# A planned graph layer on TensorE: one broadcast planned as a longer transfer, and new due times for the steps of three stages

## The chip, the cores and the metric

The kernel runs on one core of one Trainium2 chip. The metric is the device time in microseconds (us). The core's engines are TensorE (PE; its weight loads are PEld), VectorE (DVE), ScalarE (ACT), GpSimd (POOL) and SyncE (SP), which here issues every DMA. Each runs its own instructions in order and waits on semaphores for the others.

## The reference

For 64 graphs of 256 nodes and width 768, with an integer adjacency matrix per graph:

```
h   = relu(layernorm(x))
ctx = adj @ (h Wadj + badj) / deg + adj^T @ (h Wrev + brev) / rdeg + h Wself + bself
rel = sum_j adj E[adj] Wr + br deg + sum_j adj^T E[reversed adj] Wrr + brr rdeg
out = x + ctx + rel
```

All is float32.

## The kernel before

A graph (called batch here) is two halves of 128 nodes, c = 0 and 1. Three 768x768 weights times h are nine block products of 256-wide pieces; they are computed with 15 combined products after the manner of fast matrix multiplication, the left side being pieces of h ("a0" to "b2") and sums of them, the right side sums of weight blocks. To keep float32 accuracy each side is split into reduced-precision words, and a product is three passes of four matmuls of 128x384, collected in PSUM tiles (chains y, z, w in sweep one; x, v, u, t in sweep two), with a scaling by ACT between passes.

Not all right-hand words fit in SBUF at once, so the work has stages. The **opening** treats batch 0 with plain float32 matmuls ("whole", L795) while the right-hand words of sweep one are made. **Sweep one** runs 8 products for each of 62 batches and stores the partial blocks and h to DRAM. The **change** treats batch 63 with "whole" and makes the words of sweep two. **Sweep two** reloads, runs the other 7 products and the aggregation by adj ("agg", L925) and stores the result.

In sweep one each batch starts with `front1`: load x and its transposed copy xt (one tile per half, L692, L694); take means and variances (`stats`, `aggr`, `eps`, `pow`); transpose the four statistics columns into a small tile, `line` (L728); store that to DRAM, `d` (L733); read it back broadcast to all partitions, `row` (L740, 128 partitions of 2 KB, 256 KB written); then for each half `centre` on POOL (L754, h minus the row of means) and `norm` on DVE (L758, relu and scale). `norm` reads two SBUF operands. The products' left words come next (L566 to L583), and then the matmuls (L594).

The order of instructions on each engine is no loop: a planner (`Plan.schedule`) simulates the engines when the program is built. Each step has an engine, a planned duration and a due time (`rank`): the batch's start r plus a fixed number plus an entry of the table `OFFSETS`. A step is never due before a step that it needs. Among the steps that are ready in the simulation, each engine takes the one that is due first. A step's kind in the table carries "@" for batch 0, "@1" for batch 1, "$" for batch 63, "$1" for batch 62, and nothing for all others, so an entry without a mark acts on sixty batches. A DMA is planned on one queue as size/330 us, and its landing later by a constant:

```
LANDS = {"load": 2.2, "store": 1.5}
...
def on_queue(kb):
    return kb / 330.0
```

The size given for `row` was 400, so the plan has 400/330 + 2.2 = 3.41 us from issue to landing when the queue is free. Steps with `lock=True` (POOL's elementwise steps, `norm`, some of DVE's) are planned so that no POOL step and no such DVE step run together. On the chip nothing of this simulation remains but the order of each engine's instructions and the semaphores between them.

Of the kernel before, what the change touches and what calls it, by code (L numbers as in the profile page):

```python
# [102 lines left out]
    "bias adj": -238.9, "bias forward": 39.45, "bias rev": -3.35, "bias rev again": 15.06, "bias reverse": 37.57,  # L103
    "bias self": 30.03, "bias self again": 9.91, "bias01": 24.14, "bias01$1": -41.79, "bias01@1": 36.62,
# [10 lines left out]
    "degree@1": -1.22, "double adj": 35.08, "double own": -49.23, "eT": -24.29, "eps": 4.28, "eps$": 7.22,  # L115
# [1138 lines left out]
```

## Time and profile before

| | |
|---|---|
| median of 3 runs | 2445.14 us (2444.12 to 2447.47) |
| the profiled execution | 2447.47 us |
| its span, first to last instruction | 2445.7 us |
| mean granted TensorE clock | 0.999 |
| PE busy in the span | 2411.1 us (99%) |
| DVE, ACT, POOL busy | 87%, 85%, 58% |

The profiled execution is one of the three runs. Its time lies 1.8 us above its span. The page's times are from the span's start. "Idle before" is the time that an engine stood still ahead of an instruction, with what released it. A matmul's busy time overlaps that of the next one, so the number of matmuls begun in a stretch says more about PE's pace than its busy share.

### The profile page before, as it was taken

How to read it: one execution, taken by the hardware profiler on the slowest of the kernel's cores; microseconds unless marked ns; L12 is line 12 of the kernel's file. 1: busy time of each engine (PE TensorE's matmuls, PEld its weight loads, DVE VectorE, ACT ScalarE, POOL GpSimd, SP SyncE). 2: the span in 40 equal slices, each digit the busy share in tenths (PEclk: the TensorE clock that was granted, in tenths of full speed). 3: DMA queues.
4: the chain of work that ended last, by engine and by line, in shares of the span. 5: the costliest groups of instructions: out<-in, count | busy, mean ns of one | idle time of the engine just before them, and what ended most of it. 6: DMA issues, size and time to landing. Idle time of an engine off the chain costs nothing.

```text
span 2445.7 us, 43188 instructions
## 1 busy us (share of the span) xinstructions
PE 2411.1 (99%) x13510; PEld 2346.0 (96%) x13510; DVE 2133.7 (87%) x3953; ACT 2088.5 (85%) x3936; POOL 1409.2 (58%) x1230
## 2 busy tenths in 40 slices
PE   7999999999999999999999999999999999999998
PEld 4999999999999999997899999999999999999998
DVE  6888898898988889885889888888888888889888
ACT  7888888888888888888888888888888888888887
POOL 7666666666666666564555555555555555555554
PEclk9999999999999999999999999999999999999999
DMA  7788888877888888877666666666666666666664
GB/s 266 269 270 278 261 275 269 274 275 267 272 269 277 277 268 275 273 260 254 208 221 225 224 225 220 223 220 220 220 220 223 223 220 220 220 220 219 222 223 154
DMA packets 225543, 593.03 MB, mean 242 GB/s; under 512 B 25116, under 2 KB 25116, under 8 KB 225308
## 3 DMA queue, kind: packets, MB, share of 16 engines
q1 hardware_dynamic: 225308, 590.22, 71.3%
q8 instruction: 108, 1.77, 0.3%
q14 instruction: 127, 1.04, 0.1%
HBM read 366.65 MB, written 223.48 MB: 241 GB/s over the span
## 4 chain that ended last, share of the span: by engine, by line
PE 53%; ACT 1%; DVE 0%; issue 0%; DVEq 0%; ACTq 0%
PE x L594 21%; PE agg L925 14%; PE v L594 5%; PE t L594 5%; PE u L594 5%; PE whole L795 2%; PE y L594 0%; ACT agg L933 0%; PE w L594 0%; PE pr L850 0%; ACT copy L517 0%; DVE c L676 0%; PE z L594 0%; DVE c L674 0%; ACT a L893 0%
## 5 line engine op out<-in xcount | busy, mean ns | idle before, releaser
L913 POOL TENSOR_TENSOR hl<-c,hl 128x768 fp32r<-128x768 f32 x256 | 470.8, 1850 | 552.1 <-ACT hl L909 306.1
L594 PE MATMUL x<-word,left 128*128 128x384 f32 x2976 | 577.9, 335 | 1.3 <-ACT x L647 0.9
L594 PE MATMUL y<-word,left 128*128 128x384 f32 x2976 | 569.7, 335 | 1.7 <-ACT y L647 0.7
L594 PEld LDWEIGHTS y<-word,left 128*128 128x128 f32 x2976 | 519.9, 188 | 5.5 <-ACT y L647 1.7
L594 PEld LDWEIGHTS x<-word,left 128*128 128x128 f32 x2976 | 520.3, 188 | 4.5 <-ACT x L647 1.2
L925 PE MATMUL agg<-hl,a 128*128 128x384 f32 x2048 | 399.5, 337 | 4.3 <-ACT agg L933 4.3
L925 PEld LDWEIGHTS agg<-hl,a 128*128 128x128 f32 x2048 | 360.0, 188 | 5.9 <-ACT agg L933 5.2
L754 POOL TENSOR_TENSOR h<-h,row 128x768 f32<-128x768 f32 x126 | 230.2, 1848 | 151.5 <-DMA kept<-x 41.1
L594 PE MATMUL z<-word,left 128*128 128x384 f32 x1488 | 304.2, 339 | 6.0 <-ACT c L665 5.1
L594 PE MATMUL w<-word,left 128*128 128x384 f32 x1488 | 299.7, 335 | 1.3 <-DVE word L531 1.2
L594 PEld LDWEIGHTS z<-word,left 128*128 128x128 f32 x1488 | 256.0, 188 | 21.6 <-ACT c L665 17.0
L594 PEld LDWEIGHTS w<-word,left 128*128 128x128 f32 x1488 | 262.0, 188 | 3.3 <-ACT top L573 1.8
L943 DVE SCALAR_TENSOR_TENSOR c<-agg,rd,c 128x768 f32<-128x768 f32 x252 | 254.5, 1011 | 3.1 <-PE agg L925 2.2
L647 ACT ACTIVATE y<-y 128x768 f32<-128x768 f32 x248 | 195.4, 788 | 55.9 <-PE y L594 55.8
L647 ACT ACTIVATE x<-x 128x768 f32<-128x768 f32 x248 | 191.3, 793 | 27.5 <-PE x L594 26.9
L909 ACT ACTIVATE hl<-c 128x768 fp32r<-128x768 f32 x256 | 213.8, 837 | 1.0 <-DVE c L676 0.8
L573 ACT ACTIVATE top<-left 128x256 f32<-128x256 f32 x496 | 179.6, 379 | 39.2 <-DVE left L583 38.8
L583 DVE SCALAR_TENSOR_TENSOR left<-left,top 128x256 fp32r<-128x256 f32 x496 | 193.9, 410 | 2.3
L933 ACT ACTIVATE agg<-row_forward,sqd 128x768 f32<-128x768 f32 x128 | 115.4, 902 | 84.8 <-DVE c L674 84.8
L583 DVE SCALAR_TENSOR_TENSOR left<-left 128x256 fp32r<-128x256 f32 x434 | 183.5, 434 | 0.0
L676 DVE SCALAR_TENSOR_TENSOR c<-x,c 128x768 f32<-128x768 f32 x124 | 118.1, 953 | 70.2 <-ACT agg L933 68.5
L758 DVE SCALAR_TENSOR_TENSOR h<-h,row 128x768 f32<-128x768 f32 x126 | 157.8, 1253 | 0.0
(127 smaller groups left out, 4619.2 us busy)
## 6 DMA issues: line engine op xcount, KB each, us to landing
c<-kept SPq DMA_DIRECT2D x316, 384.0 KB
kept<-c SPq DMA_DIRECT2D x252, 384.0 KB
x<-in_x_dram SPq DMA_DIRECT2D x128, 384.0 KB
h<-in_x_t_dram SPq DMA_DIRECT2D x128, 384.0 KB
out_dram<-c SPq DMA_DIRECT2D x126, 384.0 KB
kept_h<-h SPq DMA_DIRECT2D x124, 384.0 KB
h<-kept_h SPq DMA_DIRECT2D x124, 384.0 KB
adj<-in_adj_dram SPq DMA_DIRECT2D x64, 512.0 KB
```

What stands on the lines that cost most here:

```text
L573: lambda: nc.scalar.activation(view(top), t(w)[:, 0].bitcast(F32), AF.Copy),
L583: lambda: nc.vector.scalar_tensor_tensor(t(w)[:, 2], t(w)[:, 1].bitcast(F32), -STEP, first(), op0=ALU.mult, op1=ALU.add), s == 1,
L594: nc.tensor.matmul(t(q)[:, half, : H // 2], t(w)[:, lw, f, :], t(r[rw])[:, f, ts(half, H // 2)], start=start and i == 0 and f == 0, stop=s ...
L647: lambda: nc.scalar.activation(view(), view(), AF.Copy, scale=scale),
L676: emit = lambda to=to, sign=sign: nc.vector.scalar_tensor_tensor(to(), view(), sign * UP, to(), op0=ALU.mult, op1=ALU.add)
L754: lambda h=h, one=one, engine=engine: engine.tensor_tensor(t(h), t(h), one(0), op=ALU.subtract),
L758: lambda h=h, one=one: nc.vector.scalar_tensor_tensor(t(h), t(h), 0.0, one(1), op0=ALU.max, op1=ALU.mult), b != 0 or part is not None,
L909: lambda: nc.scalar.activation(t(pair)[:, 0], t(o), AF.Copy, scale=LOWER),
L913: lambda: nc.gpsimd.tensor_tensor(t(pair)[:, 1], t(o), t(pair)[:, 0].bitcast(F32), op=ALU.subtract),
L925: nc.tensor.matmul(t(q)[:, half, : H // 2], t(s["a"])[:, c, k, ts(ic, P)], t(pairs[c])[:, part, ts(half, H // 2)], start=False, stop=(c == ...
L933: lambda q=q, ic=ic, row=row: nc.scalar.activation(t(q)[:, :, : H // 2], t(row).rearrange("p (k n) -> p k n", k=2), AF.Copy, scale=t(sqd)[ ...
L943: lambda q=q, to=to, ic=ic: nc.vector.scalar_tensor_tensor(to(), t(q)[:, :, : H // 2], t(rd)[:, ic, k : k + 1], to(), op0=ALU.mult, op1=AL ...
```

## The change

One number in `front1` changes: the transfer `row` is planned with 560 in place of 400 (1.70 us on the queue in place of 1.21, and 3.90 us to the landing in place of 3.41). The transfer itself stays as it is. And 523 of the 821 entries of `OFFSETS` change: 216 without a mark, 94 each of "@1" and "$1", 67 of "$" and 52 of "@". They belong to the opening, to sweep one and to the change; the entries of sweep two's products, reloads and aggregation keep their values, except those of batch 63. No instruction is added, removed or altered; all that differs is the order on each engine. The new entries were found by a search in which planned transfers land late at random. Of the diff's lines these hold the entries spoken of below:

```diff
--- before.py
+++ after.py
...
-    "c11@": 32.1, "c11@1": -1.29, "c12": 22.01, "c12$1": 29.3, "c12@": -4.98, "c12@1": 18.89, "centre0": 4.08,
...
-    "centre0$": 31.91, "centre0$1": -227.73, "centre0@": -27.75, "centre0@1": -14.15, "centre1": 6.08,
...
-    "copy of 6": -106.6, "copy of 7": 34.39, "copy of 8": -14.49, "copy of 9": -4.54, "d": -0.46, "d$": -31.64,
...
-    "left2 8@1": -28.68, "left2 9": 7.17, "left2 9$1": 9.22, "left2 9@1": -124.24, "less": 35.53, "line": 18.08,
...
-    "load raw11.1": -125.08, "load raw12.0": -1.16, "load raw12.1": -347.46, "load raw20.0": -341.35,
...
-    "low12@": -65.09, "low12@1": -2.48, "more": -34.88, "norm0": 19.03, "norm0$": -217.44, "norm0$1": -38.93,
-    "norm0@": 43.2, "norm0@1": -11.82, "norm1": -62.27, "norm1$": 17.96, "norm1$1": 29.72, "norm1@": 37.5,
...
-    "right2": 29.95, "right3": 33.09, "right4": -0.47, "right6": -45.6, "right8": -31.54, "row": 0.71, "row$": 4.41,
...
-    "x0$": 0.9, "x0$1": -71.15, "x0@": -629.88, "x0@1": -16.01, "x1": -0.52, "x1$": 2.98, "x1$1": -6.07,
-    "x1@": -413.86, "x1@1": 25.42, "xt0": 19.12, "xt0$": -1.32, "xt0$1": 18.27, "xt0@": -172.07, "xt0@1": 17.01,
-    "xt1": 9.96, "xt1$": 14.9, "xt1$1": 16.79, "xt1@": -25.36, "xt1@1": 22.17,
...
+    "c11@1": -1.29, "c12": 22.01, "c12$1": 29.3, "c12@": -4.98, "c12@1": 18.89, "centre0": -41.92, "centre0$": -37.48,
+    "centre0$1": 16.06, "centre0@": 45.41, "centre0@1": -7.3, "centre1": -68.47, "centre1$": -22.7,
...
+    "copy of 7": 40.93, "copy of 8": -39.49, "copy of 9": -32.19, "d": 12.61, "d$": 22.9, "d$1": -316.23, "d@": -7.61,
...
+    "left2 9@1": -124.24, "less": 35.39, "line": -4.43, "line$": -214.44, "line$1": -26.42, "line@": 5.09,
...
+    "load raw12.1": -253.41, "load raw20.0": -557.21, "load raw20.1": 7.87, "load raw21.0": 18.81,
...
+    "more": -75.14, "norm0": 17.76, "norm0$": -37.02, "norm0$1": -82.03, "norm0@": -22.28, "norm0@1": 22.06,
+    "norm1": -13.5, "norm1$": -264.32, "norm1$1": 29.27, "norm1@": 19.58, "norm1@1": 25.11, "out0": 13.66,
...
+    "row": 2.84, "row$": 3.1, "row$1": -37.19, "row@": -100.85, "row@1": -24.61, "rows": -60.11, "scale 1": -4.34,
...
+    "write12@": -282.31, "x0": -1.48, "x0$": 10.12, "x0$1": -67.18, "x0@": -248.59, "x0@1": -2, "x1": -0.71,
+    "x1$": -6.83, "x1$1": -0.51, "x1@": -984.16, "x1@1": 23.99, "xt0": 21.33, "xt0$": 17.66, "xt0$1": 9.26,
+    "xt0@": -65.84, "xt0@1": 15.37, "xt1": 8.41, "xt1$": 2.3, "xt1$1": 21.15, "xt1@": -610.02, "xt1@1": 16.41,
...
@@ -736,7 +735,7 @@
 
             dma(2, r - 19.0, f"d {b}", [line], [d], spread)
             dma(
-                400, r - 18.5, f"row {b}", [d], [row],
+                560, r - 18.5, f"row {b}", [d], [row],
                 lambda: nc.sync.dma_start(
                     t(row).rearrange("p k i -> p (k i)"), t(d).rearrange("k p -> (k p)").partition_broadcast(P)
                 ),
```

## Rows read from the trace of the kernel before

**Rows 1.** Stretches: length, busy time (instructions) per engine, granted clock, DMA share, GB/s.
```profile
0.00:16.15 16.15, 2.44 (x4) 1.00 (x4) 4.78 (x15) 4.45 (x8) 6.43 (x10) 1.00 0.86 318
...
100.00:1100.00 1000.00, 993.11 (x5658) 977.12 (x5657) 883.97 (x1820) 834.36 (x1647) 617.26 (x589) 1.00 0.81 271
...
1300.00:2300.00 1000.00, 1000.00 (x5754) 998.10 (x5754) 896.99 (x1540) 883.89 (x1634) 540.53 (x445) 1.00 0.66 223
```

**Rows 2.** Who waited for ACT's reads of L665, 100 to 1100 us: us, times.
```profile
  PEld z L594: 16.6, 36
```

**Rows 3.** What ACT's `top` copies (L573) waited for, 100 to 1100 us.
```profile
  DVE left L583: 38.8, 51
```

**Rows 4.** DVE's group L758, 100 to 1100 us: count, busy us, mean ns.
```profile
L758 DVE SCALAR_TENSOR_TENSOR h<-h,row 128x768 f32<-128x768 f32 x118 | 150.0, 1271 | 0.0
```

**Rows 5.** Tile `row`, 100 to 1100 us: duration ns min/median/max of `norm`.
```profile
L758 DVE SCALAR_TENSOR_TENSOR h<-h,row x118: 939/953/2285, 102.8 to 1092.5; 128x768 f32<-128x768 f32 x118
```

**Rows 6.** SP's timeline: three issues of `row` (start, duration).
```profile
723.75 0.33 SPq L740 DMA_DIRECT2D row<-d  x1
...
740.50 0.33 SPq L740 DMA_DIRECT2D row<-d  x1
...
1011.01 0.33 SPq L740 DMA_DIRECT2D row<-d  x1
```

**Rows 7.** POOL's timeline: the two `centre` steps of the same batches.
```profile
728.59 3.65 POOL L754 TENSOR_TENSOR h<-h,row 128x768 f32<-128x768 f32 x2 [2.61 <-DMA row<-d]
...
744.70 3.66 POOL L754 TENSOR_TENSOR h<-h,row 128x768 f32<-128x768 f32 x2 [1.74 <-DMA kept<-x]
...
1016.49 3.63 POOL L754 TENSOR_TENSOR h<-h,row 128x768 f32<-128x768 f32 x2 [3.82 <-DMA kept<-x]
```

**Rows 8.** DVE's timeline: the first `norm` of each, and one x load waited for.
```profile
731.32 1.74 DVE L758 SCALAR_TENSOR_TENSOR h<-h,row 128x768 f32<-128x768 f32 x1
...
748.33 0.94 DVE L758 SCALAR_TENSOR_TENSOR h<-h,row 128x768 f32<-128x768 f32 x1
...
1018.17 0.56 DVE L699 BATCH_NORM_STATS2 stats<-x 128x6 f32<-128x384 f32 x1 [0.71 <-DMA x<-in_x_dram]
1018.65 2.29 DVE L758 SCALAR_TENSOR_TENSOR h<-h,row 128x768 f32<-128x768 f32 x1
```

**Rows 9.** PE's timeline: the same point of three successive batches, and one wait.
```profile
730.23 1.58 PE L594 MATMUL z<-word,left 128*128 128x384 f32 x8
...
747.24 1.55 PE L594 MATMUL z<-word,left 128*128 128x384 f32 x8
...
763.88 1.55 PE L594 MATMUL z<-word,left 128*128 128x384 f32 x8
...
1023.89 0.97 PE L594 MATMUL z<-word,left 128*128 128x384 f32 x4 [0.80 <-ACT c L665]
```

**Rows 10.** DVE's and ACT's timelines, opening.
```profile
4.21 1.02 DVE L699 BATCH_NORM_STATS2 stats<-x 128x6 f32<-128x384 f32 x2 [3.07 <-DMA x<-in_x_dram]
...
5.39 0.96 DVE L699 BATCH_NORM_STATS2 stats<-x 128x6 f32<-128x384 f32 x2
...
12.71 0.95 DVE L754 TENSOR_TENSOR h<-h,spread 128x768 f32<-128x768 f32 x1 [5.90 <-DMA h<-in_x_t_dram]
15.14 0.95 DVE L758 SCALAR_TENSOR_TENSOR h<-h,spread 128x768 f32<-128x768 f32 x1 [1.48 <-PE spread L722]
...
7.70 0.40 ACT L716 ACTIVATE spread<-ident,cols 128x128 f32<-128x128 f32 x1 [1.72 <-POOL cols L707]
11.67 1.55 ACT L604 ACTIVATE whole<-row_adj 128x768 f32<-128x768 f32 x2 [3.57 <-DMA row_adj<-in_bias_dram]
13.15 0.68 ACT L716 ACTIVATE spread<-ident,cols 128x128 f32<-128x128 f32 x2
```

**Rows 11.** PE's timeline and a stretch as in rows 1, change.
```profile
1178.45 4.49 PE L925 MATMUL agg<-hl,a 128*128 128x384 f32 x16 [3.42 <-ACT agg L933]
...
1178.50:1182.00 3.50, 3.50 (x14) 3.30 (x15) 2.96 (x5) 3.50 (x6) 0.74 (x1) 0.67 0.78 248
```

More of the change, by code (lines that the diff above doesn't have):

```diff
@@ L91 @@
 OFFSETS = {
[1 row of a table removed]
[1 row of a table added]
     "a0+a2+b0+b2": 9.52, "a0+a2+b0+b2$1": 19.53, "a0+a2+b0+b2@1": 18.63, "a0+a2+b2": 16.61, "a0+a2+b2$1": 16.65,
[9 rows of a table removed]
-    "bias adj": -238.9, "bias forward": 39.45, "bias rev": -3.35, "bias rev again": 15.06, "bias reverse": 37.57,
-    "bias self": 30.03, "bias self again": 9.91, "bias01": 24.14, "bias01$1": -41.79, "bias01@1": 36.62,
[10 rows of a table removed]
-    "degree@1": -1.22, "double adj": 35.08, "double own": -49.23, "eT": -24.29, "eps": 4.28, "eps$": 7.22,
[97 rows of a table removed]
-    "second 9": -46.03, "second 9$1": -175.69, "second 9@1": 18.85, "self less rev": 11.6, "spread0@": -154.35,
-    "spread1@": -116.94, "sqd": -3.42, "sqd$": -2.05, "sqd$1": 55.02, "sqd@": -59.31, "sqd@1": -25.66, "stats": -6.79,
[29 rows of a table removed]
[9 rows of a table added]
+    "bias forward": 38.92, "bias rev": 8.8, "bias rev again": 15.38, "bias reverse": 37.66, "bias self": 24.27,
[11 rows of a table added]
+    "double adj": 39.89, "double own": 12.67, "eT": 9.08, "eps": -95.99, "eps$": 0.14, "eps$1": -7.48, "eps@": -32.55,
[51 rows of a table added]
+    "left2 9@1": -124.24, "less": 35.39, "line": -4.43, "line$": -214.44, "line$1": -26.42, "line@": 5.09,
[26 rows of a table added]
+    "row": 2.84, "row$": 3.1, "row$1": -37.19, "row@": -100.85, "row@1": -24.61, "rows": -60.11, "scale 1": -4.34,
[17 rows of a table added]
+    "second 8@1": 16.61, "second 9": -46.03, "second 9$1": -175.69, "second 9@1": 18.85, "self less rev": 30.15,
+    "spread0@": 3.68, "spread1@": 38.86, "sqd": -3.42, "sqd$": -0.14, "sqd$1": 55.02, "sqd@": -59.31, "sqd@1": -25.66,
+    "stats": 0.79, "stats$": 5.48, "stats$1": -11.07, "stats@": -64.04, "stats@1": -69.82, "top 10": -14.62,
[28 rows of a table added]
 }
```

269 rows, old and new, of the table OFFSETS are left out of this document.

## The prediction, on record before the result was seen

> **What bounds the kernel now.** I read the stretches first [rows 1]. The reader should see PE's count of matmuls: in 1000 us of sweep two PE begins 5754, in 1000 us of sweep one 5658. Matmuls have one shape in both, so sweep two shows PE's pace when nothing is late (173.8 ns each), and sweep one falls 96 short: 96 x 0.1738 = 16.7 us lost in that stretch. Sweep two has nothing to win, and its entries stay. What else is lost stands at the ends: the first large matmul begins only at 16.15 us, and in the change there is one gap of 3.42 us, behind which the granted clock is 0.67 over 3.5 us, part of it at the lower of the two levels (1.2 GHz), after PE had stood idle [rows 11]. So the prize is 16.7 us in sweep one and some us at either end, about 1% in all. Sweep one begins some 59 batches in the 1000 us (half of 118 `norm` steps [rows 4]), so it loses 0.28 us per batch.
>
> Next I asked whom PE waits for there. The weight loads of chain z wait 16.6 us in 36 waits for the reads by which ACT empties PSUM [rows 2], about the whole loss. ACT itself waits 38.8 us for DVE's left words before its `top` copies [rows 3]. So DVE delivers late, and the groups of DVE show one oddity: `norm` takes 1271 ns in the mean but 953 in the median and up to 2285 [rows 4, 5]. Two halves per batch share this mean; if one of them is at 0.953, the other is at (150.0 - 59 x 0.953)/59 = 1.59 us, a stretch of 0.64.
>
> Last I set three batches side by side, the same instructions on SP, POOL, DVE and PE. SP issues `row` at 723.75, 740.50 and 1011.01 [rows 6]; POOL's pair of `centre` steps starts 4.84, 4.20 and 5.48 us later and runs until 732.24, 748.36 and 1020.12 [rows 7]; the first `norm` starts at 731.32, 748.33 and 1018.65 and takes 1.74, 0.94 and 2.29 us [rows 8]. In each it ends 0.8 to 0.9 us after POOL's pair has ended: while `centre` runs, `norm` stands still. Which half is it? In the due times below `centre1` and `norm1` come first, so it is `norm1`, held by `centre0`. The three batches differ in when `row` landed. PE's answer: from 730.23 to 747.24 it needs 17.01 us, after the stretched `norm`, and from 747.24 to 763.88 16.64, after the clean one [rows 9]; 96 matmuls at 173.8 ns are 16.68. The first batch thus loses 0.37 us with a stretch of 0.79, so some 0.42 us of stretch is absorbed and the rest reaches PE; the mean stretch gives 0.64 - 0.42 = 0.22, near the 0.28 found. In the worst batch a late load of x adds to it (DVE waits 0.71 us for it [rows 8]) and PE waits 0.80 us at once [rows 9].
>
> **The change part by part.** The plan had 3.41 us from issue to landing of `row`; the chip shows 4.20 to 5.48 [rows 6, 7]. So the plan put the steps behind it 0.8 to 2 us too early. With 560 the plan has 3.90, that is 0.485 us more. Where the order keeps the slack that it had, the stretch falls to 0.64 - 0.485 = 0.16 us, below the 0.42 that is absorbed.
>
> The due times around it also move (batch start r; a step is never due before what it needs). Before: `line` r - 1.42, so `d`, `row`, `centre1` and `norm1` are all due at r - 1.42, `centre0` at r + 1.12 (with its xt load), `norm0` at r + 10.03. After: `line` at about r - 22, `d`, `row`, `centre1` and `norm1` at r - 6.39, `centre0` at r + 3.33, `norm0` at r + 8.76. The row and the first half come 5 us earlier in the order, and the two centres are due 9.7 us apart in place of 2.5, so `norm1` need not meet `centre0` at all. Due times only decide among ready steps, and all 216 unmarked entries move, so this says the direction and not the size. What must not be lost is room elsewhere, and it is there: DVE is busy for 884 of 1000 us, 37 of them the stretch (59 x 0.64), ACT for 834, the DMA engines for 81% [rows 1]; and a batch at PE's full pace is already seen with all of them in step [rows 9].
>
> Sum for sweep one: nothing lost would give 16.7 us. Batches with a late x or a landing 1.3 us over the mean keep some (2.29 - 0.485 = 1.80 us, still 0.43 over what is absorbed). I leave 3.7 of the 16.7 and take **-13.0 us**; bounds -16.7 and, with the waits unchanged, 0 (a loss is a rival below).
>
> At one place a rule speaks against this. The rows give 4.20 to 5.48 us from the issue of `row` to its first use [rows 6, 7]. The Trainium skill (DMA: Bandwidth & Descriptors, Anatomy of one DMA, SWDGE path) fits a transfer issued by GpSimd as about 2.0 us plus bytes/436 GB/s; for 256 KB that would be an estimated 2.6 us, less than the 3.41 already planned, so a longer plan would mend nothing. The trace does not agree, for this transfer from SP among others.
>
> Opening: before, the loads are due in the order x0, x1, a raw weight, another, the bias, xt0. The first lands at 4.21 and the sixth, after 8 times its bytes (384 against 3072 KB by the sizes in the code), at 12.71 us [rows 10]: 316 KB per us. Now x1 (due -985), xt1 (-601) and one raw weight (-543) precede x0 (-251), so x0 lands as 1920 KB: 4.21 + 1536/316 = 9.07. From the statistics of a second half to its ACT spread step took 7.70 - 5.39 = 2.31; from the last spread pair to `norm` 15.14 - 13.15 = 1.99; then one `centre` (0.95) and `norm` to the first matmul 16.15 - 15.14 = 1.01 [rows 1, 10]. That makes 9.07 + 2.31 + 1.99 + 0.95 + 1.01 = 15.3, and with half 1's xt there early, half 1 starts: 0.8 us sooner than 16.15. With the other spread pair ahead on ACT (0.68) it is 0.1. I take **-0.5**. If the two bias writes (1.55, their data at about 12.7) stand ahead of the spread steps on ACT, the start is 12.7 + 1.55 + 1.99 + 0.95 + 1.01 = 18.2, +2.1. Bounds -0.8 and +2.1.
>
> Change: batch 63's agg waits 3.42 us for an ACT init, and the slow clock after it costs (1 - 0.67) x 3.5 = 1.2 [rows 11]. That init's entry moves from -9.78 to -55.95, but so do its neighbours'; no row prices the new order. Bounds -4.6 (gap gone) and +4.6 (another as large); I take **0**.
>
> Row size 400 to 560 itself costs nothing on the chip: SP issues the same descriptors. The end of sweep two keeps its entries: 0.
>
> Sum: -13.5. The profiled execution took 2447.47 us, so it would take 2434.0. The median of the runs is 2.3 us below that execution: 2445.14 - 13.5 = **2431.6**. I call 0.2%, 4.9 us, the least that can be told from no change; the three runs lie within 3.4 us.
>
> **The rivals.**
> 1. *Another wait takes half of it.* With the row early, chain z waits for some other read. For it: 51 waits of `top` on DVE and 36 on L665 lie close together [rows 2, 3], and all re-ranked steps share four in-order engines. Against: the clean batch. Half of 16.7 is 8.35: 2445.1 - 8.35 - 0.5 = 2436.3, faster.
> 2. *The change doesn't do what it says.* The 0.485 us are too few against 0.8 to 2, or the search traded them away, and `norm` is stretched as before: only the -0.5 stays, 2444.6, same. By the page of the Trainium skill named above this is what would come. The trace bears that out little: the landing is past the plan in each of the three batches.
> 3. *Slower: the second half comes late.* `xt0`, and with it `centre0`, is due 2.2 us later (r + 3.33) while `norm0` is due 1.3 us earlier. If its load lands late, POOL stands with `centre0` at the head, and behind it the sums for the left words, and all "a" products wait. For it: late loads do occur, and PE feels them [rows 8, 9]. Against: `centre0` is still due 5.4 us ahead of `norm0` (8.9 before). It decides from the loss per batch on: today's is 0.28 us; above 0.28 + 5.4/60 = 0.37 the kernel is slower by more than 0.2%. At 0.5 us in 60 batches it loses 30 in place of 16.7: +13.3 - 0.5, 2458.
>
> **How the numbers follow.** Forecast (2422 to 2436) 0.56; rival 1 (2436 to 2440) 0.16; rival 2 (2440 to 2449) 0.14; rival 3 0.14. The predicted time is the forecast's. The lower end takes all three bounds, 2445.1 - 16.7 - 0.8 - 4.6 = 2423.0, and one for the runs: 2422. The upper end takes in rivals 1 and 2: 2448. Outside lie rival 3 and some for a better result than the bounds. Faster by over 0.2%: 0.56 + 0.16 = 0.72; within: 0.14; slower: 0.14.
>
> **What would show it.** In 1000 us of sweep one some 5730 matmuls in place of 5658. The group `norm` of L758 at a mean below 1.1 us with a maximum under 2. PE's waits on L665 under 5 us. `row` issued over 8 us ahead of the first `norm` (7.57, 7.83 and 7.64 now [rows 6, 8]), or the two `centre` steps apart, so that POOL no longer overlaps it. The first "whole" matmul between 15 and 16.2 us. Wrong would be: `norm` at its 0.95 and sweep one as slow as now (then the stretch was no cause, or rival 1); a stretch as now (rival 2); POOL or DVE waiting for xt loads (rival 3); or a new gap in the change larger than 3.4 us.

## The result and the profile after

| | before | after |
|---|---|---|
| median of 5 runs | 2445.14 us (2443.86 to 2447.47) | 2432.9 us (2430.81 to 2434.54) |
| ratio of the times, 95% interval | | 0.9949 (0.9935 to 0.9964) |
| profiled execution, span | 2447.47, 2445.7 us | 2432.9, 2431.1 us |

The kernel is faster by 12.2 us; 13.5 were forecast. One execution of e8 below took 4866.89 us, twice as long as any other; no ratio counts it. In the kernel after, line numbers are one lower (`norm` is L757, `centre` L753, `row` L739). The stretches of [rows 1], the 58 us behind the opening, and two stretches behind gaps of PE:

```profile
0.00:16.15 16.15, 2.08 (x4) 1.18 (x4) 4.18 (x14) 4.31 (x8) 5.26 (x10) 1.00 0.86 307
16.15:74.00 57.85, 55.02 (x173) 34.80 (x174) 47.91 (x79) 51.47 (x77) 48.83 (x34) 0.97 0.71 262
67.40:71.00 3.60, 3.59 (x13) 3.60 (x14) 3.37 (x9) 2.91 (x7) 2.21 (x3) 0.62 0.82 279
100.00:1100.00 1000.00, 997.38 (x5724) 989.43 (x5723) 865.65 (x1831) 841.34 (x1667) 623.34 (x591) 1.00 0.83 275
1166.80:1170.30 3.50, 3.50 (x13) 3.50 (x14) 3.40 (x5) 3.50 (x6) 1.48 (x2) 0.58 0.89 299
1300.00:2300.00 1000.00, 1000.00 (x5764) 998.24 (x5763) 897.29 (x1538) 884.78 (x1643) 545.41 (x449) 1.00 0.65 223
```

In sweep one PE begins 5724 matmuls in 1000 us, 66 more than before: 66 x 0.1738 = 11.5 us. That is nearly all of the gain. What PE's weight loads and ACT's `top` copies wait for in that stretch answers to [rows 2, 3]:

```profile
PEld w L593 <- ACT c L664: 3.4, 8, 1.0
...
PEld z L593 <- ACT c L664: 0.7, 2, 0.5
```

```profile
ACT top L572 <- DVE left L582: 6.6, 14, 0.9
```

ACT waits 6.6 us for left words in place of 38.8, PE 4.1 us for ACT's reads in place of 16.6. The chain that the prediction followed upward has let go at each link. But its first link, the stretched `norm`, is still there. The group of `norm` and the tile `row`, 100 to 1100 us, beside [rows 4, 5]:

```profile
L757 DVE SCALAR_TENSOR_TENSOR h<-h,row 128x768 f32<-128x768 f32 x120 | 139.7, 1165 | 0.0
```

```profile
L757 DVE SCALAR_TENSOR_TENSOR h<-h,row x120: 946/1112/2592, 99.6 to 1094.5; 128x768 f32<-128x768 f32 x120
L753 POOL TENSOR_TENSOR h<-h,row x119: 1832/1851/1870, 101.4 to 1091.5; 128x768 f32<-128x768 f32 x119
...
its engine sat idle before it (us, times) until:
  DMA h<-in_x_t_dram: 112.9, 33
```

The mean fell from 1271 to 1165 ns and the maximum rose to 2592. POOL seems to wait 112.9 us for loads of xt, but all transfers here take turns on eight semaphores, and the profile can name another transfer than the one waited for. By the DMA packets it is `row`: in the 28 batches between 100 and 1060 us where a load of xt is named ahead of the pair, the pair starts 0.41 to 0.61 us after the last of `row`'s 128 packets, just as where `row` is named (0.42 to 0.52 us, three batches). Three batches show why a stretch costs less. SP's `row`, POOL's pair and DVE's first `norm` (beside [rows 6 to 8]):

```profile
765.22 0.32 SPq L739 DMA_DIRECT2D row<-d  x1
...
781.98 0.32 SPq L739 DMA_DIRECT2D row<-d  x1
```

```profile
620.17 3.66 POOL L753 TENSOR_TENSOR h<-h,row 128x768 f32<-128x768 f32 x2 [4.66 <-DMA h<-in_x_t_dram]
...
770.51 3.66 POOL L753 TENSOR_TENSOR h<-h,row 128x768 f32<-128x768 f32 x2 [4.81 <-DMA h<-in_x_t_dram]
...
787.51 3.67 POOL L753 TENSOR_TENSOR h<-h,row 128x768 f32<-128x768 f32 x2 [4.42 <-issue]
```

```profile
622.45 0.41 DVE L578 TENSOR_TENSOR left<-a2+b,top 128x256 fp32r<-128x256 f32 x1
622.78 1.87 DVE L757 SCALAR_TENSOR_TENSOR h<-h,row 128x768 f32<-128x768 f32 x1
...
625.23 1.12 DVE L757 SCALAR_TENSOR_TENSOR h<-h,row 128x768 f32<-128x768 f32 x1
...
772.78 2.21 DVE L757 SCALAR_TENSOR_TENSOR h<-h,row 128x768 f32<-128x768 f32 x1
...
789.73 2.25 DVE L757 SCALAR_TENSOR_TENSOR h<-h,row 128x768 f32<-128x768 f32 x1
```

And PE at the same point of successive batches (beside [rows 9]):

```profile
621.83 1.55 PE L593 MATMUL z<-word,left 128*128 128x384 f32 x8
...
638.50 1.58 PE L593 MATMUL z<-word,left 128*128 128x384 f32 x8
...
771.84 1.58 PE L593 MATMUL z<-word,left 128*128 128x384 f32 x8
...
788.79 1.58 PE L593 MATMUL z<-word,left 128*128 128x384 f32 x8
...
805.78 1.55 PE L593 MATMUL z<-word,left 128*128 128x384 f32 x8
```

The first `norm` still ends 0.8 us after POOL's pair (772.78 + 2.21 against 770.51 + 3.66). But a stretch of 0.92 us (1.87 - 0.95) now costs nothing: 638.50 - 621.83 = 16.67, PE's full pace. One of 1.26 costs 16.95 - 16.68 = 0.27, one of 1.30 costs 16.99 - 16.68 = 0.31. So some 0.95 us of stretch is absorbed in the new order, where the old one absorbed some 0.42. All batches between 100 and 1060 us bear this out (read off the traces; the loss is PE's time for the 96 matmuls from the first `norm` on, less 16.68 us). In the kernel before, 18 batches have a stretch of 0.70 to 0.95 us and lose 0.38 us in the mean, none under 0.27; in the kernel after, the four such batches lose nothing.

The rest of the gain and loss, by the time at which PE begins its k-th matmul, read off the two traces (13510 matmuls in each, in the same order up to the 5452nd and again from the 6204th; "spread" is the same quantity in the four profiled kernels with each order on every engine, apart from one POOL step in some, used in the experiments):

| part (matmuls) | before | after | gain | spread before; after |
|---|---|---|---|---|
| first large matmul (k = 4) | 16.15 | 16.94 | -0.8 | 15.25 to 16.60; 16.29 to 17.12 |
| up to the end of the opening (k = 188) | 74.07 | 76.03 | -2.0 | 73.77 to 76.59; 75.57 to 77.37 |
| sweep one (188 to 5900) | 1008.92 | 996.03 | +12.9 | |
| change (5900 to 6500) | 135.34 | 134.52 | +0.8 | 135.34 to 136.62; 134.23 to 135.21 |
| sweep two (6500 to the last) | 1220.77 | 1218.17 | +2.6 | 1220.15 to 1220.77; 1218.17 to 1219.98 |

The first row is part of the second. The profiled pair differs by 14.6 us, 2.3 more than the medians, because the profiled execution of the kernel before lies that much above its median.

### The profile page after: what moved, and what is told of

Read it like the earlier page. It is cut to its first block, busy times and chain, and to the rows that moved or that the text cites. A ratio compares the mean times of both kernels' runs of the same rounds, so it can differ in the third digit from the quotient of the medians.

```text
span 2431.1 us, 43342 instructions
## 1 busy us (share of the span) xinstructions
PE 2400.7 (99%) x13510; PEld 2347.3 (97%) x13510; DVE 2107.5 (87%) x3953; ACT 2083.6 (86%) x3936; POOL 1412.5 (58%) x1230
## 4 chain that ended last, share of the span: by engine, by line
PE 96%; ACT 1%; DVE 1%; DMA 1%; issue 0%; SPq 0%; POOL 0%; DVEq 0%; ACTq 0%; POOLq 0%
PE x L593 21%; PE y L593 21%; PE agg L924 14%; PE w L593 11%; PE z L593 10%; PE v L593 5%; PE u L593 5%; PE t L593 5%; PE whole L794 2%; DMA kept<-c 0%; DVE right L520 0%; DVE word L530 0%; DMA x<-in_x_dram 0%; ACT copy L516 0%; ACT agg L932 0%
## 5 line engine op out<-in xcount | busy, mean ns | idle before, releaser
L753 POOL TENSOR_TENSOR h<-h,row 128x768 f32<-128x768 f32 x126 | 231.0, 1851 | 214.3 <-DMA h<-in_x_t_dram 115.0
L593 PE MATMUL v<-word,left 128*128 128x384 f32 x744 | 149.0, 334 | 0.0
```

Source lines behind the costliest of these rows:

```text
L593: nc.tensor.matmul(t(q)[:, half, : H // 2], t(w)[:, lw, f, :], t(r[rw])[:, f, ts(half, H // 2)], start=start and i == 0 and f == 0, stop=s ...
L753: lambda h=h, one=one, engine=engine: engine.tensor_tensor(t(h), t(h), one(0), op=ALU.subtract),
```

## The experiments

The runs went in three sets, each on one chip with its own runs of the kernel before (medians 2446.12, 2446.84, 2446.99 us); ratios are to those. The last column is the time in which PE does the 4700 matmuls from the 300th to the 5000th, in the profiled execution; at sweep two's pace they would take 4700 x 0.1738 = 816.9 us.

| kernel | set | median, us | ratio (interval) | 300 to 5000, us |
|---|---|---|---|---|
| before | | 2445.14 | 1 | 830.06 |
| after | | 2432.9 | 0.9949 (0.9935 to 0.9964) | 818.58 |
| e1, before, half centre | 1 | 2430.07 | 0.993 (0.9914 to 0.9947) | 816.19 |
| e2, before, 560 | 1 | 2443.48 | 0.9989 (0.998 to 0.9999) | 820.23 |
| e3, after, 400 | 1 | 2442.04 | 0.9984 (0.9974 to 0.9994) | 821.67 |
| e4, 560 and sweep one's entries | 1 | 2469.25 | 1.009 (1.0073 to 1.0106) | 816.81 |
| e5, before, long centre | 2 | 2449.04, one run | | 830.32 |
| e6, after, long centre | 2 | 2436.16, one run | | 818.62 |
| e7, after, old batch 0 | 2 | 2437.56 | 0.9963 (0.9952 to 0.9975) | 817.47 |
| e8, after, half centre | 2 | 2432.23 | 0.993 (0.9903 to 0.9958) | 817.77 |
| e9, before, late pair | 3 | 2472.51 | 1.011 (1.0087 to 1.0133) | 853.95 |
| e10, after, late pair | 3 | 2438.41 | 0.9965 (0.9954 to 0.9975) | 822.01 |
| e11, after, 720 | 3 | 2466.56 | 1.0083 (1.0065 to 1.01) | 841.36 |
| e12, after, x0 second | 3 | 2431.34 | 0.9943 (0.9927 to 0.996) | 817.98 |

**Is it the meeting of `norm` with the second `centre`?** e1 and e8 shorten the second half's `centre` to three of the six column blocks, in the kernel before and in the one after; the order on each engine stays.

```diff
+if c == 0 and b in regular:
+    few = t(row)[:, 0:1, :].to_broadcast([P, 3, P])
+    engine.tensor_tensor(t(h)[:, :3, :], t(h)[:, :3, :], few, op=ALU.subtract)
+else:
     engine.tensor_tensor(t(h), t(h), one(0), op=ALU.subtract)
```

> The kernel before, its order of steps untouched; only POOL's second centre of each batch of sweep one subtracts in half of its columns, so that it takes about 0.93 us in place of 1.85 (left out: the mean in three of six column blocks of half 0). The theory that the first norm stands still while this centre runs, and that what is over 0.42 us of it reaches PE, expects: the first norm at 0.95 to 1.3 us nearly always, sweep one's loss of 16.7 us per 1000 down to 3 or less, and 2428 to 2434 us. The rival, that the stretched norm only goes along with an order that is slow for other reasons (ACT's reads behind left words), expects 2443 to 2447 us and the waits on L665 as they are.

The half step took 1.02 us in place of 1.85, no `norm` exceeded 1.26, and ACT's `top` copies waited 2.0 us for left words. The stretch 100 to 1100 us and the tile `row` of e1:

```profile
100.00:1100.00 1000.00, 998.91 (x5733) 991.37 (x5732) 860.09 (x1834) 845.50 (x1670) 572.29 (x591) 1.00 0.82 277
```

```profile
L762 DVE SCALAR_TENSOR_TENSOR h<-h,row x120: 939/950/1257, 103.6 to 1097.6; 128x768 f32<-128x768 f32 x120
...
L755 POOL TENSOR_TENSOR h<-h,row x59: 1006/1017/1039, 102.1 to 1069.3; 128x384 f32<-128x384 f32 x59
```

0.83 us less on POOL, which is 62% busy [rows 1], gave 16 us: all of what sweep one lost. The cause that the prediction named is shown.

> The changed kernel, order untouched, with the second centre in half of its columns (left out: the mean in three of six column blocks of half 0). If the stretch that is left there (0.31 us in the mean, some batches over 1 us) still costs PE, sweep one gains what it still loses, 1 to 4 us: 2428 to 2432 us. The rival, that the rest of the loss in the changed sweep one has other causes (loads of x and xt, the last batches), expects 2432 to 2434 us.

In the kernel after, the same edit takes 0.8 us off the 4700 matmuls, and its ratio can't be told from that of the kernel after (three executions; their median is 2431.38 us, the table's counts the fourth). Between the two expectations it doesn't decide, but there is little of this cause left to take.

e5 and e6 lengthen it instead: behind the full second `centre` POOL runs that half step as well.

```diff
+engine.tensor_tensor(t(h), t(h), one(0), op=ALU.subtract)
+if c == 0 and b in regular:
+    few = t(row)[:, 0:1, :].to_broadcast([P, 3, P])
+    engine.tensor_tensor(t(h)[:, :3, :], t(h)[:, :3, :], few, op=ALU.subtract)
```

> The kernel before, order untouched; POOL's second centre of each batch of sweep one subtracts a second time in half of its columns, about 1.0 us more (changed: the mean is taken off twice in three of six column blocks of half 0). If the first norm stands still behind the second centre and 0.42 us of that is absorbed, each batch loses about 1.0 us more: 60 us, 2495 to 2515 us, the first norm at about 2.6 us in the mean. The rival, that PE's waits come from the order and POOL has room (it is busy 62% there), expects under 2465 us.

> The same 1.0 us added to the second centre of the changed kernel (the mean is taken off twice in three of six column blocks of half 0). If its order has 0.96 us more from the issue of row to the first norm and absorbs some 0.95 us of stretch in place of 0.42, it loses far less than the kernel before does with the same edit: 0.3 to 0.5 us a batch, 2450 to 2465 us. The rival, that the changed order has no more slack than the old one and only meets the centre less often, expects 1.0 us a batch, 2490 us or more.

The longer step costs almost nothing: 2449.04 - 2446.84 = 2.2 us in e5, and e6 stands at 2436.16 / 2446.84 = 0.9956 of before where the kernel after has 0.9949, 1.8 us (one run each). For both that is a miss: 2495 us and 2450 us were the least expected. POOL's and DVE's timelines of e5 show it:

```profile
712.92 3.66 POOL L753 TENSOR_TENSOR h<-h,row 128x768 f32<-128x768 f32 x2 [2.59 <-PE y L594]
716.65 1.61 POOL L756 TENSOR_TENSOR h<-h,row 128x384 f32<-128x384 f32 x1
```

```profile
715.67 1.72 DVE L761 SCALAR_TENSOR_TENSOR h<-h,row 128x768 f32<-128x768 f32 x1
```

`norm` ends at 717.39, 0.8 us after the pair (716.58) and before the added step (718.26), which took 1.61 us in place of 1.02. In 54 of the 62 batches of e5 it is so: `norm` ends 0.81 to 0.93 us after the pair and the step behind takes 1.61 us or more. So `norm` is held by the one POOL instruction that runs when it comes, and then goes ahead of the next. What e1 removed was thus the end of that one instruction, not POOL time as such.

**The size or the due times?** e2 is the kernel before with 560, e3 the one after with 400, e11 the one after with 720.

```diff
-                400, r - 18.5, f"row {b}", [d], [row],
+                560, r - 18.5, f"row {b}", [d], [row],
```

> The kernel before with the planned size of row alone changed from 400 to 560; all due times as before. In the order of a batch the first norm then stands one left step (0.33 us) later on DVE, SP's and POOL's orders are the same. The theory that the planned size gives the slack expects the mean stretch of the first norm to fall from 0.64 to about 0.3 us, under the 0.42 that is absorbed, and 2430 to 2437 us. The rival, that the new due times made the gain and not the size, expects the row to land as late as before and 2441 to 2447 us.

The size alone moves steps past each other: in the middle of sweep one e2 gains 9.8 of the 13.2 us that stand above PE's pace, and the first `norm`'s mean stretch falls to 0.38 us (0.67 before, over all batches whose `row` is issued between 100 and 1050 us), near the 0.3 expected. But it is 5.0 us behind at matmul 300 (the first word product begins 2.05 us later, and behind it PE waits for ACT several times, 1.16 us at the longest), and between matmuls 5000 and 5900 it loses 7.6 us more, in batches with gaps of PE such as these:

```profile
1018.66 1.66 PE L594 MATMUL w<-word,left 128*128 128x384 f32 x8 [0.95 <-ACT c L665]
...
1066.89 1.68 PE L594 MATMUL y<-word,left 128*128 128x384 f32 x8 [1.05 <-ACT y L604]
```

By the medians it is 2.6 us faster than before, 0.1% (this profiled execution, 2447.57, lies 4 us above its median). So the stretch went as the first expectation had it, and the time came out in the range of its rival.

> The changed kernel with the planned size put back to 400; all due times new. The norms then stand one left step (about 0.4 us) earlier on DVE. The theory that the size gives the slack expects a stretch like that of the kernel before and most of sweep one's gain gone, 2441 to 2446 us. The theory that the new due times carry it, since there the row is issued 8.7 us ahead of the first norm in place of 7.7 and some 0.9 us of stretch are absorbed in place of 0.4, expects a longer stretch (mean first norm 1.5 to 1.7 us) and 2432 to 2437 us.

The due times alone gain 8.4 us in the middle and lose in the change: 140.56 us between matmuls 5900 and 6500, 6 more than after, with an agg gap of 4.12 us. The time is that of the first expectation, but for another reason: most of sweep one's gain is kept (the first `norm` takes 1.42 us in the mean). Each half does most of the middle by itself; only together do they keep it at the ends.

e4 takes 560 and the 282 new entries that belong to sweep one's steps, and leaves those of the opening and the change as before.

```diff
-                400, r - 18.5, f"row {b}", [d], [row],
+                560, r - 18.5, f"row {b}", [d], [row],
...
-    "centre0": 4.08,
+    "centre0": -41.92,
-    "norm1": -62.27,
+    "norm1": -13.5,
```

> The planned size 560 and the new due times of sweep one's steps alone (282 entries); opening and change keep the old ones. In the changed kernel the 188th matmul began 2.0 us later than before, so if the stages add, this gains sweep one's part without that loss: 2429 to 2433 us, below the changed kernel. The rival, that sweep one's order is good only with the opening that it was searched with, expects 2435 us or more.

The rival held: the middle is the best that any table of due times gave, 816.81, and the kernel is 23 us slower. The opening's second part and the change:

```profile
16.15:74.00 57.85, 49.69 (x145) 28.92 (x146) 43.70 (x69) 45.50 (x63) 41.49 (x28) 0.96 0.62 220
1100.00:1200.00 100.00, 83.66 (x323) 58.80 (x322) 51.29 (x71) 72.66 (x122) 48.40 (x32) 0.98 0.61 211
```

PE is 16.1 us behind at matmul 188 and takes 155.2 us over the 600 matmuls of the change, 20 more than before. The stages' gains don't add. That sweep one's due times also rank its steps against the word steps at either end would explain it; no run separates this.

> The changed kernel with the planned size at 720 in place of 560 (4.38 us planned from issue to landing, close to the 4.2 to 5.5 seen). If only the truth of the planned landing counted, this would be as good or better, 2430 to 2433 us. If the due times were tuned to 560 and any other plan loses at the ends of the stages, as 400 did, 2436 to 2446 us, with sweep one's middle no worse.

Here no `norm` is stretched at all, and the kernel is slower than before, its middle too: both expectations missed. The tile `row`, and PE's waits, 100 to 1100 us:

```profile
L757 DVE SCALAR_TENSOR_TENSOR h<-h,row x116: 941/951/959, 104.5 to 1090.2; 128x768 f32<-128x768 f32 x116
```

```profile
PE w L593 <- ACT c L664: 9.4, 30, 0.7
```

PE's weight loads wait 19.0 us for the same reads, and DVE 72.9 us, 113 times, for ACT's `top` copies (45.4 us, 99 times, in the kernel after). A longer plan isn't a safer one: with these due times it gives another order with a wait of its own, the kind of wait that rival 1 of the prediction feared, and here it costs more than all that was gained.

**How much lateness does each order absorb?** e9 and e10 put a short POOL step that needs `row` (one block, 0.46 us) ahead of the first `centre` in the 62 batches of sweep one, so that both `centre` steps end later.

```diff
+if c == 1 and b in regular:
+    few = t(row)[:, 2:3, :]
+    engine.tensor_tensor(t(h)[:, :1, :], t(h)[:, :1, :], few, op=ALU.subtract)
 engine.tensor_tensor(t(h), t(h), one(0), op=ALU.subtract)
```

> The kernel before, order untouched; ahead of POOL's first centre of each batch of sweep one a short extra subtract of one column block, which also needs row, about 0.46 us (changed: the mean is taken off twice in one of six column blocks of half 1). It acts like a row that lands 0.46 us later. If the first norm stands still until the second centre ends and 0.42 us of its stretch is absorbed, nearly all of it reaches PE: about 0.4 us a batch, 24 us, 2465 to 2473 us. The rival, that DVE and ACT have room for it, expects under 2455 us.

> The same 0.46 us ahead of the first centre in the changed kernel (the mean is taken off twice in one of six column blocks of half 1). With its longer distance from row to the first norm and 0.95 us of stretch absorbed it should lose little: the mean stretch goes from 0.31 to about 0.75, some batches go over, 0 to 0.15 us a batch, 2433 to 2442 us. The rival, that its slack is no larger than that of the kernel before, expects 0.4 us a batch, 2455 us or more.

e9 is 25.5 us slower than before: 25.5 / 62 = 0.41 us a batch for 0.46 put in, nearly all of it. Its `norm` group, 100 to 1100 us, and PE's wait over the whole span (in the kernel before it is 5.1 us, 16 times):

```profile
L761 DVE SCALAR_TENSOR_TENSOR h<-h,row 128x768 f32<-128x768 f32 x116 | 176.2, 1519 | 0.2
```

```profile
PE z L594 <- ACT c L665: 27.7, 44, 1.3
```

e10's ratio lies 0.0016 above that of after, 4 us or 0.06 a batch; the two intervals overlap. The same lines of e10:

```profile
L760 DVE SCALAR_TENSOR_TENSOR h<-h,row 128x768 f32<-128x768 f32 x120 | 154.3, 1287 | 0.6 <-POOL h L755 0.3
```

```profile
PE z L593 <- ACT c L664: 1.0, 3, 0.5
```

The first `norm` is stretched by 0.55 us in the mean, not far below the 0.67 of the kernel before (the group's mean also has the second `norm`, which takes 1.10 in this order and 0.95 in the old one), and PE waits 1.0 us in place of 27.7. This tells two accounts of the gain apart: with nearly as much stretch as before, e10 keeps 830.06 - 822.01 = 8.1 of the 11.5 us that after gains in those 4700 matmuls. Its five batches with a stretch of 0.70 to 0.95 us lose nothing either. The new order gains mostly by bearing the stretch, and less by shortening it.

**The opening.** e7 gives the kernel after the 52 old entries of batch 0, e12 only one of them, so that x0 is loaded second.

```diff
-    "x0@": -248.59, "x1@": -984.16, "xt0@": -65.84, "xt1@": -610.02,
+    "x0@": -629.88, "x1@": -413.86, "xt0@": -172.07, "xt1@": -25.36,
...
```

> The changed kernel with the 52 entries of batch 0 alone put back (x0 and x1 first among the loads again). If the first large matmul began 0.8 us later for x0's place in the queue, it begins at about 16.15 us again and the rest stays: 2431 to 2433 us. The rival, that the stages were planned together, expects a loss in the opening where words of sweep one come late, 2436 us or more.

The first large matmul begins at 15.20, but PE then waits 3.6 us for ACT and is at matmul 188 only at 80.12, 4.1 us later than after. The rival held; starting sooner need not be finishing sooner.

```diff
-    "x0@": -248.59,
+    "x0@": -629.88,
```

> The changed kernel with one entry put back, that of batch 0's first load of x, so that it is the second load in place of the fourth. Arithmetic as in the prediction: its data come 1152 KB earlier, 3.6 us, the bias then bounds the start, and the first large matmul begins at 14.5 to 15.5 us in place of 16.9. If the start bounds the opening, 1.5 us are won: 2431 to 2432 us. If the words of sweep one bound it (PE already waits 2.0 us for one behind the large matmuls), PE only waits longer for them: 2432.5 to 2434 us.

```profile
13.53 3.57 PE L1464 MATMUL whole<-raw,h 128*128 128x384 f32 x5 [3.24 <-ACT whole L1273]
```

PE's timeline of e12 (its lines are numbered otherwise): the start is 3.4 us earlier than after and matmul 188 comes at 72.22, 3.8 earlier. Here the words do come sooner with the start: the first word product begins at 65.18, 2.2 us earlier than after, again behind a wait of 2.0 us for its word. The other 1.6 us go with the granted clock, 1.00 over the 3.6 us from 65.15 where the kernel after had 0.62. The profiled execution keeps 3.5 of it to the last matmul; the ratio gives 1.5 us, as the first expectation had it, but its interval overlaps that of after. It has the lowest time of the kernels that do the whole work, but it can't be told from the kernel after.

## Why the prediction was right, and where not

- **Time and sign.** 2431.6 against 2432.9: the sum of -13.5 was -12.2. In the profiled pair sweep one's term, -13.0, measured -12.9, and the whole -14.6: the opening came out 2.5 us worse than its term, the change and sweep two together 3.4 better. That the sum fits so closely is in part luck, and so is sweep one's term: its size was a share of the loss left by judgement, and the way in which it was to come about failed in part, as follows.
- **The cause** (`norm` stands still while the second `centre` runs, left words come late, PE's z chain waits for ACT) is shown by e1, which shortens only that `centre` and gains all of sweep one's loss, by e5, where more POOL time behind it costs next to nothing, and by e9, which adds to the stretch and loses what was added.
- **The step that failed: how the cause would be mended.** "The stretch falls to 0.64 - 0.485 = 0.16 us, below the 0.42 that is absorbed", and the two `centre` steps apart. POOL still runs them as a pair. The first `norm`'s mean stretch fell from 0.67 to 0.30 us (read off the traces batch by batch, 56 and 57 batches), not to 0.16, and the second, clean before, now takes 1.11. The distance from the issue of `row` to the first `norm` did grow, from 7.74 to 8.72 us in the mean, as the sign of over 8 us had it. But the landing came later and spread: `row`'s last packet ends 4.38 us after the issue before (3.6 to 5.0) and 4.67 after (2.8 to 6.4). So half of the batches are clean (under 0.1 us) and others are stretched by up to 1.6; the prediction took a mean from a mean. What grew besides is the room: 0.42 to about 0.95 us absorbed. Both signs that the prediction set for `norm` (mean under 1.1, maximum under 2) failed while the time came true. The figure of 0.42 was taken for a constant of the kernel; it belongs to the order, and the diff changes the order. In the old order the left words for a0+a1+b0+b and a2+b stand right behind the first `norm`; in the new one a2+b's go ahead of it and a0+a1+b0+b's behind the second. Which of the moved steps makes the room wasn't separated.
- **Rival 2** (nothing changes) is out. The Trainium skill (DMA: Bandwidth & Descriptors, Anatomy of one DMA, SWDGE path), weighed in the prediction, would have had a longer plan mend nothing. The runs don't agree: e2, which changes only that number, takes 9.8 us out of 4700 matmuls, though its whole time gains 0.1% alone.
- **Rival 3** (xt late) didn't come. The 33 waits that the profile puts down to xt are, by the packets, waits for `row`. The sign was ill chosen: the name that a wait carries has to be tested against the packets first. The prediction's own rows have such names: [rows 7] give a store of x for two of the three pairs, and these too start some 0.5 us after `row`'s last packet.
- **Rival 1** took no half: the waits of PE's weight loads on L664 are 4.1 us, under the 5 that were set. e11 shows that it was possible.
- **The opening was mis-sized:** -0.5 forecast, +0.8 at the first large matmul and +2.0 at matmul 188, inside the bound of +2.1 but not by its cause (over four traces of each order the means differ by 0.7 and 1.5). The order of loads was as read. These are the rows of the start, from DVE's, ACT's and PE's timelines (beside [rows 10]):

```profile
9.97 1.02 DVE L698 BATCH_NORM_STATS2 stats<-x 128x6 f32<-128x384 f32 x2 [4.74 <-DMA x<-in_x_dram]
...
14.90 0.95 DVE L753 TENSOR_TENSOR h<-h,spread 128x768 f32<-128x768 f32 x1 [3.46 <-PE spread L721]
15.89 0.95 DVE L757 SCALAR_TENSOR_TENSOR h<-h,spread 128x768 f32<-128x768 f32 x1
```

```profile
12.33 0.99 ACT L715 ACTIVATE spread<-ident,cols 128x128 f32<-128x128 f32 x3 [0.60 <-POOL cols L706]
...
13.22 1.53 ACT L603 ACTIVATE whole<-row_adj 128x768 f32<-128x768 f32 x2
```

```profile
12.79 2.08 PE L721 MATMUL spread<-spread 128*128 128x256 f32 x4 [12.79 <-ACT spread L715]
16.94 1.62 PE L794 MATMUL whole<-raw,h 128*128 128x384 f32 x2 [2.08 <-issue]
...
67.41 2.21 PE L593 MATMUL w<-word,left 128*128 128x384 f32 x8 [2.04 <-DVE word L530]
69.41 2.59 PE L593 MATMUL y<-word,left 128*128 128x384 f32 x8
```

  x0 came at 9.97, not 9.07 (+0.9); the four matmuls that spread the statistics of both halves ran as one group of 2.08 us with `centre` behind them, so that 2.57 us passed from the last spread step to `centre` (12.33 to 14.90) where 1.99 were put (+0.6). The two bias writes stood behind the spread steps, so the case of +2.1 didn't arise. What the sum left out is the far end of the opening: the first word product waits 2.04 us for a DVE word, and the granted clock is 0.62 over the next 3.6 us. The prediction priced when the opening starts, not when its words are ready; e7 shows that the two can part, e12 that they need not.
- **The change: 0 forecast, 0.8 us gained.** The gap of [rows 11] is still there, 3.44 us for the same kind of step at 1166.73, with a clock of 0.58 behind it.
- **Sweep two: 0 forecast, 2.6 us gained in the profiled pair.** The order of its steps is the same in both kernels. Four profiled kernels with the order of before average 1220.4, four with that of after 1219.1; so half of the 2.6 is the spread of executions, and some 1.3 us remain whose cause is open.

## What to carry to other kernels

A group whose mean lies far above its median can be a wait in disguise, one that the profile counts as busy time: look for what runs on the neighbour engine at its ends, and test it by shortening that neighbour's step, as e1 did. How much lateness an order bears is a property of the order: measure it before and after by adding a known lateness (0.41 us a batch against 0.06 here), and don't carry the figure of one order into the other. Due times of neighbouring stages belong together; half a table can be worse than none (e4), and a plan without any stretch can be slower (e11). Where many transfers share semaphores, the profile's name for a wait can be wrong: set the step's start beside the transfer's last packet.

## What the runs showed of the hardware

- Two POOL instructions back to back don't hold a waiting DVE instruction for both: `norm` ended 0.8 us after the one that ran when it came, and the POOL step behind took 1.61 us in place of 1.02 (e5, 54 batches). The Trainium skill (SBUF — State Buffer, SBUF: two separate sides) says that whichever starts first holds the port pair that the two engines share for the whole instruction, and the other blocks. The trace agrees: `norm` has two SBUF operands and stands still until that instruction's end. It shows besides that the waiting one comes next.
- The same idle time of PE did not always cost the clock. With the same order, the first word product came after 2.04 us of waiting in the kernel after and after 2.04, 2.42 and 2.79 in e8, e6 and e10. In the kernel after the granted clock was 0.62 over the next 3.6 us (the stretch from 67.40 above), part of it at the lower level (1.2 GHz). The like stretches of e8 and of e6 show 1.00, that of e10 0.69, in this order:

```profile
68.50:72.10 3.60, 3.57 (x20) 3.60 (x21) 3.40 (x9) 3.50 (x8) 2.23 (x4) 1.00 0.86 284
```

```profile
69.00:72.60 3.60, 3.57 (x21) 3.60 (x22) 3.40 (x9) 3.51 (x8) 2.22 (x3) 1.00 0.89 253
```

```profile
68.70:72.30 3.60, 3.56 (x15) 3.59 (x16) 3.41 (x9) 2.93 (x7) 2.21 (x3) 0.69 0.80 273
```

  In 3.6 us PE began 13 matmuls in the kernel after, and 20 and 21 at the full clock: 7 or 8 x 0.1738 = 1.2 to 1.4 us. What decides between them wasn't found.
- Executions with one and the same order on every engine begin the first large matmul between 15.25 and 16.60 us (the order of before, apart from one POOL step). A difference of 0.8 us in the opening of two traces is within that.
